# A graph layer's last two stages: relus over two chunks at once, fixed places for t, and an early merge of moments

## The chip, the cores and the metric

The kernel runs on one core of one Trainium2 chip. The metric is the time of one execution on the device, in microseconds (us). A core has a tensor engine (TensorE; PE in the profile, with weight loads as PEld), a vector engine (VectorE, DVE), a scalar engine (ScalarE, ACT), GpSimd (POOL) and a sync engine (SP) that only issues transfers. Each engine works through its own instructions in order and waits on semaphores for the others. Sixteen DMA engines move data between the chip's memory (HBM) and the on-chip SBUF; SP, ACT and POOL issue those transfers from their own queues. Matrix products land in PSUM, from where DVE or ACT take them.

## What is computed

A layer norm with relu, one graph convolution of the GIN kind with two dense layers and two batch norms, and a residual. There are N = 12500 nodes of 256 features, 200000 edges sorted by their target, and a hidden width of 512.

```python
h = jnp.maximum(_layernorm(x, axis=-1), 0.0)
src, dst = (edge_index[0], edge_index[1])
agg = jax.ops.segment_sum(h[src], dst, num_segments=N)
z = (1.0 + eps_gin) * h + agg
t = jnp.dot(z, W1) + b1
t = jax.nn.relu(_batchnorm(t, g1, bt1))
conv_out = jnp.dot(t, W2) + b2
out = jax.nn.relu(_batchnorm(conv_out + h, g2, bt2))
x = x + out
```

A batch norm needs mean and variance over all nodes, so nothing behind it can start before the last node's values are there. That splits the kernel into three stages.

## The kernel before

The nodes are cut into 25 chunks: chunks 0 to 23 have 512 nodes, chunk 24 has 212. Inside the last two stages features lie on the 128 partitions and nodes run along the free dimension; a chunk of y is then a tile of 128 x 2 x 512 (`DC` = 2 halves of the 256 features), a chunk of t is four slices of 128 x 512 (`HC` = 4).

**First stage** (to about 1944 us). For each group of 12 x 128 edges POOL gathers the rows of h with indirect transfers (L529), PE adds them up by target, and the first dense layer follows. Its results, still without batch norm, go to a table in HBM, `t_tab`; h itself, transposed, goes to `h_cols`. The statistics of t are gathered in `st1`. The first eight loads of t slices are already issued in this stage. The change leaves this stage alone.

**The y stage** (about 1947 to 2117 us; the loop `for g in range(NCH)` after `t_load` is defined). For each chunk g:
- ACT applies batch norm 1 and relu to the four slices in place (L809), after their loads have landed;
- ACT issues the load of h for chunk g+3 into y's tile `yT` (L791), and from chunk 1 on one load of a chunk of x for the last stage (`x_load`, `soon`), into ten buffers `xr` and into tiles that are no longer needed (`gtb`, `gta`, `dstT`, `srcT`, `w1s`). Twenty of the 25 chunks of x are loaded here, chunk 24 among them, in a spare part of `dstT`;
- PE multiplies with W2, 8 products in 16 passes (L823);
- SP issues the four loads of chunk g+2's slices (L788). The pool `tin` has `SLICES` = 8 buffers, two chunks' worth, so that each load waits until PE has used the slice two chunks back;
- DVE adds the product to h in `yT` (L830) and takes the statistics of the sum into `st2` (L831).

Then `norm` (L298 to L309) makes scale `sc2` and offset `of2` of batch norm 2: it aggregates the 25 chunks' statistics for each half of the features and does a few tiny operations. `merge` (L282) is a helper that the first batch norm already uses: it aggregates the chunks that are there early and writes the result back as if it were one chunk.

**The tail** (about 2119 us to the end). First SP loads the five chunks of x that had no room before: four into a pool `xmore` that takes the place of `tin`, and chunk 23 into `w2s` (L776). Then for each chunk, 0 to 24 in order, ACT applies scale, offset and relu to the two halves of `yT` in place (L848), PE transposes to rows of nodes with 8 transposes into one PSUM tile `po` (L859), DVE adds that to the chunk of x, in place (L862), and SP stores it to the output (L774; chunk 24 in two stores through `carry`, L353). A store waits for its add; SP's queue holds first the five loads, then the 26 stores in this order.

The order of instructions on each engine in these two stages is that of the code.

Of the kernel before, what the change touches and what calls it, by code (L numbers as in the profile page):

```python
# [15 lines left out]
P = 128  # L16
R = 4
# [9 lines left out]
ACT_PACE = (9, 1)  # L27
SPARE = 4
XIN = 10
XMORE = 4  # L30
SLICES = 8


COPIES = 2
# [6 lines left out]
def kernel(  # L41
# [253 lines left out]
    def norm(pool, st, mv, count, gamma, beta, bias, tag, upto=1):  # L295

        for f in range(count):
            nc.vector.bn_aggr(mv[:, f, :], st[:, f, upto - 1 :, :].rearrange("p g s -> p (g s)"))  # L298
# [10 lines left out]
        nc.vector.tensor_add(of, of, beta)  # L309
        return sc, of  # L310
# [21 lines left out]
    def fast():  # L332
# [24 lines left out]
        with ExitStack() as fs:  # L357
# [398 lines left out]


            late = fs.enter_context(tc.tile_pool(name="late", bufs=1, reuse_waits="tile"))
            yT = [late.tile([P, DC, w * R], F32, name=f"yT{g}") for g, (_, w) in enumerate(chunks)]

            xin = fs.enter_context(tc.tile_pool(name="xin", bufs=XIN, reuse_waits="tile"))
            xrs = {}
# [13 lines left out]
                    eng.dma_start(sb, side)  # L776

            fs.enter_context(tc.manual_schedule())
            with tc.tile_pool(name="tin", bufs=SLICES, side="right", reuse_waits="tile") as tin, tc.tile_pool(
                name="ps_y", bufs=4, space=PSUM  # L780
            ) as ps_y:
                tis = {}

                def t_load(g):
                    n = chunks[g][1] * R
                    for f in range(HC):
                        tis[g, f] = tin.tile([P, CH], F32, name="ti")
# [12 lines left out]
                places += [rows_in(dstT), rows_in(srcT.bitcast(F32)), rows_in(w1s.rearrange("p a b -> p (a b)"))]  # L800
                soon = [(NCH - 1, rows_in(dstT, R * D, len(parts[NCH - 1])))]
                soon = [*enumerate(places)] + soon

                for g in range(2):
                    t_load(g)
                for g in range(NCH):
                    n = chunks[g][1] * R
                    for f in range(HC):
                        nc.scalar.activation(  # L809
                            tis[g, f][:, :n], tis[g, f][:, :n], AF.Relu, bias=of1[:, f : f + 1],  # L810
                            scale=sc1[:, f : f + 1],
                        )
                    for k in range(4) if g == 0 else (g + 3,):
                        if k < NCH:
                            h_load(nc.scalar, k)
                    if soon and g:
                        x_load(nc.scalar, *soon.pop(0))
                    pys = [ps_y.tile([P, CH], F32, name="py") for _ in range(DC)]
                    steps = [(f, d) for f in range(HC) for d in range(DC)]
                    if g == NCH - 1:  # L820
                        steps.sort(key=lambda fd: fd[1])
                    for f, d in steps:
                        nc.tensor.matmul(  # L823
                            pys[d][:, :n], lhsT=w2s[:, f, d * P : (d + 1) * P], rhs=tis[g, f][:, :n],
                            start=(f == 0), stop=(f == HC - 1),
                        )
# [10 lines left out]
            with tc.tile_pool(name="xmore", bufs=XMORE, side="right", reuse_waits="tile") as xmore, tc.tile_pool(  # L837
                name="ps_o", bufs=3, space=PSUM
            ) as ps_o:
                got = len(xrs) - 1  # L840
                assert got + XMORE + 1 == NCH - 1
                for g in range(got, got + XMORE):
                    x_load(nc.sync, g, xmore.tile([P, R, D], F32, name="xr"))
                x_load(nc.sync, NCH - 2, rows_in(w2s.rearrange("p a b -> p (a b)")))
                for g in range(NCH):
                    xt = xrs[g]
                    for d in range(DC):
                        nc.scalar.activation(  # L848
                            yT[g][:, d, :], yT[g][:, d, :], AF.Relu, bias=of2[:, d : d + 1], scale=sc2[:, d : d + 1]
                        )  # L850
                    po = ps_o.tile([P, R, D], F32, name="po")
                    full = len(parts[g]) == R
                    for c, rows in parts[g]:
                        for d in range(DC):
                            if full:
                                nodes = yT[g][:, d, :].rearrange("p (q c) -> p c q", c=R)[:, c, :]
                            else:
                                nodes = yT[g][:, d, c * P : c * P + rows]
                            nc.tensor.transpose(po[:rows, c, d * P : (d + 1) * P], nodes, ident)  # L859
                    for c0, c1, rows in pieces(g):  # L860
                        if c0 < c1:
                            nc.vector.tensor_add(xt[:rows, c0:c1, :], po[:rows, c0:c1, :], xt[:rows, c0:c1, :])  # L862
                    by_four(nc.sync, xt, out, g, store=True)

# [250 lines left out]
```

## Time and profile before

| what | us |
|---|---|
| median of three runs (2167.28 to 2169.49) | 2168.06 |
| the profiled execution, whole | 2167.07 |
| its span, from the first to the last record | 2165.2 |
| y stage: first product to last product | 1947.9 to 2115.9 |
| batch norm 2: last statistics to first relu | 2116.7 to 2119.5 |
| tail: first relu to last relu | 2119.5 to 2154.5 |
| first store issued, last store issued | 2124.2, 2156.9 |

All places in time below are counted from the start of the span. The profile is a record of one execution: each instruction with its start and length, and, worked out from semaphores, what released an engine that had been idle. A group of equal instructions is shown with its busy time and the mean length of one; what stands behind the second bar is the time for which the engine sat idle just before them, and who ended that. Lengths of neighbours on one engine can overlap a little, so the distance from one to the next may be less than the mean length. "DMA share" is the mean busy share of the 16 DMA engines. In this execution the tensor engine was granted 0.87 of its full clock over the whole span, 1.00 in the y stage.

### The profile page before, as it was taken

The page shows a single profiled execution, that of the slowest core. Times are in us where ns is not written, and L with a number is a line of the kernel's source. Part 1 is how long each engine was busy: PE and PEld are TensorE (multiplying, and loading weights), DVE is VectorE, ACT ScalarE, POOL GpSimd, SP SyncE. Part 2 cuts the span into 40 slices and gives each one's busy share as a digit, 9 for nine tenths or more (in the row PEclk, how much of TensorE's full clock was granted, in tenths as well). Part 3 has the DMA queues.
Part 4 walks back from the last instruction along what each step waited for, and adds up shares of the span by engine and source line. Part 5 has one row for each costly group of instructions (what it writes and reads, how often), then busy time and mean ns, then how long its engine had stood idle before and what let it go on. Part 6 is the DMA issues. An engine that isn't in the chain of part 4 may idle for free.

```text
span 2165.2 us, 20953 instructions
## 1 busy us (share of the span) xinstructions
PE 1599.3 (74%) x4874; PEld 981.8 (45%) x4874; DVE 803.0 (37%) x1292; ACT 408.3 (19%) x772; POOL 1464.3 (68%) x1555
## 2 busy tenths in 40 slices
PE   4666767777777777777777777776777777779996
PEld 3454545554444444444444444443444454444445
DVE  5556657552223223223223223323322322323336
ACT  4666667530000000000000000000000000014446
POOL 7777777777777777777777777777777777760000
PEclk9778988988878988889788988898988878999999
DMA  6676877554444444444444444444444444449977
GB/s 198 211 222 223 250 230 233 176 144 126 131 129 135 115 130 136 121 123 136 121 128 132 120 129 131 128 119 131 136 118 126 134 118 123 135 119 314 309 235 288
DMA packets 153845, 349.87 MB, mean 162 GB/s; under 512 B 33564, under 2 KB 63916, under 8 KB 153710
## 3 DMA queue, kind: packets, MB, share of 16 engines
q0 software_dynamic: 74048, 202.28, 33.7%
q1 hardware_dynamic: 42102, 82.38, 11.6%
q10 hardware_dynamic: 37560, 63.76, 8.4%
q8 instruction: 41, 0.67, 0.1%
q14 instruction: 94, 0.77, 0.1%
HBM read 284.29 MB, written 64.00 MB: 161 GB/s over the span
## 4 chain that ended last, share of the span: by engine, by line
POOL 32%; DMA 20%; PE 19%; issue 18%; ACT 6%; DVE 4%; ACTq 0%; DVEq 0%; POOLq 0%
POOL gt L529 28%; PE py L823 8%; PE ps L585 7%; DMA gtb<-h_tab,srcT 6%; DMA gta<-h_tab,srcT 6%; DMA gt<-h_tab,srcT 4%; POOL gta L529 3%; PE ph L626 3%; DMA gt<-in_x_dram,srcT 3%; ACT gt L406 2%; DVE stg L395 2%; ACT yT L848 2%; PE pz L605 2%; ACT gta L406 1%; DMA gta<-in_x_dram,srcT 1%
## 5 line engine op out<-in xcount | busy, mean ns | idle before, releaser
L529 POOL DMA_INDIRECT gt<-h_tab,srcT x708 | 670.7, 947 | 215.9 <-issue 211.0
L585 PE MATMUL ps<-gt,oh 128*128 128x256 f32 x1848 | 619.0, 458 | 242.7 <-DMA gt<-h_tab,srcT 211.6
L585 PEld LDWEIGHTS ps<-gt,oh 128*128 128x128 f32 x1848 | 364.5, 219 | 490.8 <-DMA gt<-h_tab,srcT 341.9
L637 DVE BATCH_NORM_STATS2 st<-ph 128x6 f32<-128x512 f32 (+1 forms) x98 | 67.8, 692 | 946.1 <-PE ph L626 946.0
L529 POOL DMA_INDIRECT gta<-h_tab,srcT x315 | 298.0, 946 | 96.1 <-issue 47.0
L585 PE MATMUL ps<-gta,oh 128*128 128x256 f32 x822 | 258.8, 435 | 69.4 <-DMA gta<-h_tab,srcT 68.5
L639 ACT COPY ts<-ph 128x512 f32<-128x512 f32 (+1 forms) x24 | 13.5, 561 | 1433.7 <-DVE st L637 1433.7
L605 PE MATMUL pz<-at,zs 128*128 128x256 f32 (+1 forms) x524 | 202.3, 528 | 92.5 <-ACT zs L592 85.6
L529 POOL DMA_INDIRECT gt<-in_x_dram,srcT x216 | 204.4, 946 | 65.8 <-issue 60.7
L585 PEld LDWEIGHTS ps<-gta,oh 128*128 128x128 f32 x822 | 161.3, 214 | 171.9 <-DMA gta<-h_tab,srcT 135.3
L585 PE MATMUL ps<-gtb,oh 128*128 128x256 f32 x416 | 162.2, 507 | 96.7 <-DMA gtb<-h_tab,srcT 75.4
L564 DVE TENSOR_TENSOR oh<-col,dstT 128x1536 f32<-128x1536 f32 x131 | 227.6, 1737 | 0.0
L626 PE MATMUL ph<-zc,w1s 128*128 128x512 f32 (+1 forms) x392 | 199.8, 639 | 26.6 <-DVE hc L515 25.7
L605 PEld LDWEIGHTS pz<-at,zs 128*128 128x128 f32 x524 | 139.7, 273 | 135.0 <-ACT zs L592 102.4
L529 POOL DMA_INDIRECT gtb<-h_tab,srcT x160 | 151.5, 947 | 48.8 <-PE ps L585 29.3
L823 PE MATMUL py<-ti,w2s 128*128 128x512 f32 (+1 forms) x400 | 167.9, 582 | 2.9 <-ACT ti L809 2.9
L585 PEld LDWEIGHTS ps<-gtb,oh 128*128 128x128 f32 x416 | 91.3, 243 | 149.7 <-DMA gtb<-h_tab,srcT 76.9
L616 DVE TENSOR_TENSOR zc<-pz,zc 128x512 f32<-128x512 f32 (+8 forms) x187 | 92.6, 518 | 121.7 <-PE pz L605 91.1
L626 PEld LDWEIGHTS ph<-zc,w1s 128*128 128x128 f32 x392 | 79.5, 206 | 92.9 <-issue 53.9
L823 PEld LDWEIGHTS py<-ti,w2s 128*128 128x128 f32 x400 | 75.8, 190 | 95.1 <-issue 86.6
L406 ACT ACTIVATE gt<-gt,nbg,rsg 128x256 f32<-128x256 f32 x216 | 108.1, 586 | 9.0 <-DVE nbg L404 9.0
L809 ACT ACTIVATE ti<-ti,of,sc 128x512 f32<-128x512 f32 (+1 forms) x100 | 76.1, 797 | 86.7 <-DMA ti<-t_tab 73.3
(119 smaller groups left out, 984.7 us busy)
## 6 DMA issues: line engine op xcount, KB each, us to landing
t_tab<-ts ACTq DMA_DIRECT2D x96, 256.0 KB
ti<-t_tab SPq DMA_DIRECT2D x96, 256.0 KB
one_s<-h_tab SPq DMA_DIRECT2D x1280, 1.0 KB
one_a<-h_tab ACTq DMA_DIRECT2D x1280, 1.0 KB
xt<-in_x_dram SPq DMA_DIRECT2D x24, 512.0 KB
h_tab<-ht ACTq DMA_DIRECT2D x24, 512.0 KB
h_cols<-hc SPq DMA_DIRECT2D x24, 512.0 KB
zc<-h_cols SPq DMA_DIRECT2D x24, 512.0 KB
```

The costliest lines, as they stand in the source:

```text
L395: nc.vector.bn_stats(st[:, c : c + 2, :].rearrange("p c s -> p (c s)"), two.rearrange("p c d -> p d c"),)
L406: nc.scalar.activation(slot(to, c), slot(v, c), AF.Relu, bias=nb[:, c : c + 1], scale=rs[:, c : c + 1])
L529: nc.gpsimd.indirect_dma_start(out=slot(ga, t - t0)[:rows], out_offset=None, in_=x if i < LEAD else h_tab, in_offset=bass.IndirectOffsetOn ...
L564: nc.vector.tensor_tensor(ohs[i][:, :n, :], col[:, :P].unsqueeze(1).to_broadcast([P, n, P]), dstT[:, t0 : t0 + n].unsqueeze(2).to_broadcas ...
L585: nc.tensor.matmul(ps, lhsT=oh[:rows, j, :], rhs=fetched[:rows], start=(j == order[0]), stop=(j == order[-1]))
L605: nc.tensor.matmul(pz[:, d, :n], lhsT=zs[:, d * P : (d + 1) * P], rhs=at[:, :n], start=True, stop=True)
L616: nc.vector.tensor_add(side, pz[:, :, a - lo : b - lo], side)
L626: nc.tensor.matmul(ph[:, :n], lhsT=w1s[:, d, f * P : (f + 1) * P], rhs=zc[c][:, d, :n], start=(d == 0), stop=(d == DC - 1),)
L637: nc.vector.bn_stats(st1[:, f, c, :], ph[:, :n])
L809: nc.scalar.activation(tis[g, f][:, :n], tis[g, f][:, :n], AF.Relu, bias=of1[:, f : f + 1], scale=sc1[:, f : f + 1],)
L823: nc.tensor.matmul(pys[d][:, :n], lhsT=w2s[:, f, d * P : (d + 1) * P], rhs=tis[g, f][:, :n], start=(f == 0), stop=(f == HC - 1),)
L848: nc.scalar.activation(yT[g][:, d, :], yT[g][:, d, :], AF.Relu, bias=of2[:, d : d + 1], scale=sc2[:, d : d + 1])
```

## The change

Five edits, all in the y stage and the tail.

1. y's tiles hold two chunks each (`twos`, 128 x 2 x 1024; `yT[g]` is one half of one), and the tail relus two chunks in one operation per half of the features. Chunks 0 and 1 are still done singly.
2. t's slices have two fixed places of four slices (`rings`) for even and odd chunks in place of a pool of eight. Chunk 24's four short slices go to other places: one of their own, `col_i`, and `st1`, which is no longer needed.
3. Four late chunks of x are loaded into the two places as chunks 22 and 23 leave them, in the y stage, in place of the pool `xmore`. Chunk 23's still goes to `w2s`.
4. The statistics of the first 23 chunks are merged after chunk 22's, and batch norm 2 aggregates three entries, the merged one and the last two.
5. The tail begins with chunk 24: DVE applies scale and offset (no relu) to it, and its add takes the relu along. Chunk 0's add and store are split into two halves.

```diff
@@
-            yT = [late.tile([P, DC, w * R], F32, name=f"yT{g}") for g, (_, w) in enumerate(chunks)]
+            twos = [late.tile([P, DC, 2 * CH], F32, name=f"yT{k}") for k in range(NCH // 2)]
+            yT = [twos[g // 2][:, :, g % 2 * CH : (g % 2 + 1) * CH] for g in range(NCH - 1)]
+            yT.append(late.tile([P, DC, chunks[-1][1] * R], F32, name="yT_last"))
@@
-            with tc.tile_pool(name="tin", bufs=SLICES, side="right", reuse_waits="tile") as tin, tc.tile_pool(
-                name="ps_y", bufs=4, space=PSUM
-            ) as ps_y:
+            with tc.tile_pool(name="ps_y", bufs=4, space=PSUM) as ps_y:
+                tin = fs.enter_context(tc.tile_pool(name="tin", bufs=1, side="right", reuse_waits="tile"))
+                rings = [tin.tile([P, HC, CH], F32, name=f"ti{k}") for k in range(2)]
+                short = chunks[-1][1] * R
+                dead = st1.rearrange("p f g s -> p (f g s)")
+                lasts = [tin.tile([P, short], F32, name="ti_last"), col_i.bitcast(F32)]
+                lasts += [dead[:, k * short : (k + 1) * short] for k in range(HC - 2)]
@@
-                        tis[g, f] = tin.tile([P, CH], F32, name="ti")
+                        tis[g, f] = rings[g % 2][:, f, :] if g < NCH - 1 else lasts[f]
@@
                     if g + 2 < NCH:
                         t_load(g + 2)
+                    if g >= NCH - 3 and g < NCH - 1:
+                        for k in range(2):
+                            x_load(nc.sync, len(xrs) - 1, rows_in(rings[g % 2].rearrange("p f n -> p (f n)"), k * R * D))
+                    if g == NCH - 2:
+                        merge(st2, mv2, DC, NCH - 2)
@@
-            sc2, of2 = norm(late, st2, mv2, DC, g2c, bt2c, b2c, "2")
+            sc2, of2 = norm(late, st2, mv2, DC, g2c, bt2c, b2c, "2", NCH - 2)
@@
-                got = len(xrs) - 1
-                assert got + XMORE + 1 == NCH - 1
-                for g in range(got, got + XMORE):
-                    x_load(nc.sync, g, xmore.tile([P, R, D], F32, name="xr"))
                 x_load(nc.sync, NCH - 2, rows_in(w2s.rearrange("p a b -> p (a b)")))
-                for g in range(NCH):
+                for k, g in enumerate([NCH - 1, *range(NCH - 1)]):
                     xt = xrs[g]
                     for d in range(DC):
-                        nc.scalar.activation(
-                            yT[g][:, d, :], yT[g][:, d, :], AF.Relu, bias=of2[:, d : d + 1], scale=sc2[:, d : d + 1]
-                        )
+                        sc, of = sc2[:, d : d + 1], of2[:, d : d + 1]
+                        if k == 0:
+                            nc.vector.tensor_scalar(
+                                yT[g][:, d, :], yT[g][:, d, :], sc, of, op0=OP.mult, op1=OP.add
+                            )
+                        elif g < 2:
+                            nc.scalar.activation(yT[g][:, d, :], yT[g][:, d, :], AF.Relu, bias=of, scale=sc)
+                        elif g % 2 == 0:
+                            two = twos[g // 2][:, d, :]
+                            nc.scalar.activation(two, two, AF.Relu, bias=of, scale=sc)
@@
+                    if k == 1:
+                        side = out[chunks[g][0] : chunks[g][0] + CH, :].rearrange("(p c) d -> p c d", c=R)
+                        for c in range(0, R, 2):
+                            nc.vector.tensor_add(xt[:, c : c + 2, :], po[:, c : c + 2, :], xt[:, c : c + 2, :])
+                            nc.sync.dma_start(side[:, c : c + 2, :], xt[:, c : c + 2, :])
+                        continue
                     for c0, c1, rows in pieces(g):
-                        if c0 < c1:
+                        if c0 == c1:
+                            continue
+                        if k == 0:
+                            nc.vector.scalar_tensor_tensor(
+                                xt[:rows, c0:c1, :], po[:rows, c0:c1, :], 0.0, xt[:rows, c0:c1, :],
+                                op0=OP.max, op1=OP.add,
+                            )
+                        else:
                             nc.vector.tensor_add(xt[:rows, c0:c1, :], po[:rows, c0:c1, :], xt[:rows, c0:c1, :])
                     by_four(nc.sync, xt, out, g, store=True)
```

The order of instructions that results, engine by engine: POOL's is the same. On DVE five instructions of the merge stand between chunk 22's and chunk 23's adds. On SP, before the tail's stores, two x loads wait for chunk 22's products and two for chunk 23's, and w2s's waits for chunk 24's. The loads of h on ACT stand where they stood and now write two runs of 512 elements per partition in place of one of 1024. ACT has 26 relus in the tail in place of 50.

More of the change, by code (lines that the diff above doesn't have):

```diff
@@ L29 @@
 XIN = 10
-XMORE = 4
-SLICES = 8
 COPIES = 2
@@ L758, in fast @@
             late = fs.enter_context(tc.tile_pool(name="late", bufs=1, reuse_waits="tile"))
-            yT = [late.tile([P, DC, w * R], F32, name=f"yT{g}") for g, (_, w) in enumerate(chunks)]
+            assert NCH % 2 and all(w == P for _, w in chunks[:-1])
+            twos = [late.tile([P, DC, 2 * CH], F32, name=f"yT{k}") for k in range(NCH // 2)]
+            yT = [twos[g // 2][:, :, g % 2 * CH : (g % 2 + 1) * CH] for g in range(NCH - 1)]
+            yT.append(late.tile([P, DC, chunks[-1][1] * R], F32, name="yT_last"))
             xin = fs.enter_context(tc.tile_pool(name="xin", bufs=XIN, reuse_waits="tile"))
@@ L832, in fast @@
                 assert not soon
[L834 to L843 removed]
+            sc2, of2 = norm(late, st2, mv2, DC, g2c, bt2c, b2c, "2", NCH - 2)
+            with tc.tile_pool(name="ps_o", bufs=3, space=PSUM) as ps_o:
+                assert len(xrs) == NCH - 1 and NCH - 2 not in xrs
                 x_load(nc.sync, NCH - 2, rows_in(w2s.rearrange("p a b -> p (a b)")))
[L845 removed]
+                for k, g in enumerate([NCH - 1, *range(NCH - 1)]):
                     xt = xrs[g]
                     for d in range(DC):
[L848 to L850 removed]
+                        sc, of = sc2[:, d : d + 1], of2[:, d : d + 1]
[8 more added lines that the diff above has]
+                            nc.scalar.activation(two, two, AF.Relu, bias=of, scale=sc)
                     po = ps_o.tile([P, R, D], F32, name="po")
```

## The prediction

> **What bounds the kernel now.** I read first the chain of waits over the last hundred microseconds, because every edit lies in the last two stages: y (PE product L823, DVE add and statistics L830/L831) and the output tail (ACT relu L848, PE transposes L859, DVE add L862, SP store L774).
>
> ```profile
> 2059.78 56.10 PE py L823 x140
> ...
> 2116.70 1.43 DVE mv L298 x2
> ...
> 2119.54 27.02 ACT yT L848 x39
> ...
> 2147.08 6.47 ACT yT L848 x9
> 2153.59 1.13 PE po L859 x7
> ...
> 2155.88 0.74 DVE dstT L862 x2
> ```
>
> Columns are start, length, engine, tile, line. Until 2115.9 PE alone is the chain: the y stage runs at PE's pace. Then 3.6 us of statistics, and from 2119.5 the tail runs at ACT's pace. The last link is the short chunk 24, which comes after everything else.
>
> Second, the groups by form: busy time and mean ns of one stand behind the bar.
>
> ```profile
> L848 ACT ACTIVATE yT<-yT,of,sc 128x512 f32<-128x512 f32 x48 | 34.0, 803 | 1.1 <-DVE of L309 1.1
> L809 ACT ACTIVATE ti<-ti,of,sc 128x212 f32<-128x212 f32 x4 | 2.3, 563 | 3.5 <-DMA ti<-t_tab 3.5
> L558 ACT ACTIVATE zc<-zc,gin 128x1024 f32<-128x1024 f32 x5 | 5.7, 1132 | 0.0
> L862 DVE TENSOR_TENSOR xr<-po,xr 128x1024 f32<-128x1024 f32 x14 | 17.0, 1223 | 5.4 <-PE po L859 5.3
> L298 DVE BATCH_NORM_AGGREGATE mv<-st 128x2 f32<-128x150 f32 x2 | 1.5, 794 | 0.0
> L298 DVE BATCH_NORM_AGGREGATE mv<-st 128x2 f32<-128x12 f32 x4 | 0.8, 208 | 0.1
> ```
>
> 48 relus take 34.0 us, 0.708 each in a row, so 1.41 per chunk; DVE needs 1.22.
>
> Third, the tail in windows of 2 us (stretch, length, busy PE, PEld, DVE, ACT, POOL, granted clock, DMA share, GB/s), since a faster ACT meets the stores next.
>
> ```profile
> 2128.00:2130.00 2.00, 1.66 (x11) 1.47 (x12) 1.81 (x2) 2.00 (x4) 0.00 (x0) 1.00 1.01 399
> 2144.00:2146.00 2.00, 1.82 (x15) 1.63 (x15) 1.81 (x2) 2.00 (x4) 0.00 (x0) 1.00 0.91 363
> 2148.00:2150.00 2.00, 1.82 (x13) 1.63 (x14) 1.81 (x2) 2.00 (x4) 0.00 (x0) 1.00 0.91 348
> 2158.00:2160.00 2.00, 0.00 (x0) 0.00 (x0) 0.00 (x0) 0.00 (x0) 0.00 (x0) 0.50 0.56 193
> ```
>
> ACT is never idle, but the DMA engines are already at 91 to 101%. While the first four chunks (added 1.21 us apart) were a backlog, 2125.2 to 2132.4, they moved 395 GB/s in mean of the finer windows; later they waited a little for ACT. So ACT is the bound by a small margin, and a store of 524,288 bytes costs 524288/395e9 = 1.33 us of DMA: that is the next bound.
>
> Last, the DMA queues in the middle of y (1980 to 2020): packets, MB, share of 16 engines.
>
> ```profile
> q1 hardware_dynamic: 3407, 6.20, 47.6%
> q10 hardware_dynamic: 1624, 5.92, 42.2%
> ```
>
> q1 is SP's t slices in rows of 2 KB, q10 is ACT's h and x loads in rows of 4 KB. Together 90%: the y stage has one tenth of its DMA time to spare.
>
> **The change part by part.**
>
> *Norm 2.* merge takes 23 chunks out of the last aggregate. Two aggregates of 150 elements (794 ns) become two of 18; between the rows 128x12 (208) and 128x150 the slope is 4.2 ns, so 233 each. On the chain 1.43 us become about 0.45: gain 1.0 (0.9 to 1.1). The merge costs 2 x 0.74 (144 elements: 758 ns) + 0.07 + 0.16 + 0.31 = 2.0 us on DVE, once, after chunk 22's statistics at 2108.05. There DVE idles 4.1 us until PE ends chunk 23, so nothing; without that cover it would be 2.0. ACT's first relu then starts at 2118.5, not 2119.5.
>
> *t's places and x's late chunks.* The slices keep their depth: a load of chunk g+2 waits for the same two products of chunk g. Chunk 24's four short slices get places of their own and wait for none; they gain nothing, because PE reaches them at 2112.8. Four x loads leave the head of the tail (SP issued five at 2114.9 to 2117.3) for the ends of chunks 22 and 23, 2102 to 2112.6, where the DMA share is 0.26 and lower. Behind them on SP stand only w2s's load and the stores, wanted no earlier than 2120.9. Cost nothing; at worst, if all four still stood before the first store, 4 x 1.33 = 5.3 us of DMA would, as before, end near 2123.5, and the gain of the first store below (0.3) would be gone.
>
> *h loads.* y's tiles of two chunks cut each row of 4 KB in two of 2 KB. From the queue rows: q1 took 0.476 x 640 engine-us for 6.20 MB = 49.1 per MB, q10 0.422 x 640 / 5.92 = 45.6. So 0.524 MB x 3.5 = 1.8 engine-us more per chunk, 0.11 us over 16 engines: DMA goes from 6.17 to 6.29 of PE's 6.86 us. Hidden, zero. At the upper end a half row could cost as much as a whole one: see the third rival.
>
> *Relu in pairs.* 4 single relus (chunks 0, 1) stay, 22 of 1024 elements replace 44. No row shows this form. Low end 1.13 us (L558, same size, one operand fewer), high end 1.41 (two single ones, no gain). From 212 to 512 elements the same operation grows by (803-563)/300 = 0.80 ns each, so 803 + 512 x 0.80 = 1.21, less the 0.10 by which neighbours overlap (803 against 708): I take 1.12, 2.24 per two chunks. ACT falls to 1.12 per chunk, under DVE's 1.22 and the store's 1.33. The price: chunk 2 waits for a relu of two chunks.
>
> *Chunk 24 first, chunk 0 in halves.* Chunk 24 gets its scale from DVE, two of about 0.4 us (L597: 286 ns at 84 elements, 393 at 180), four transposes, two adds of 0.42 (L862: 415) with the relu folded in; its two stores go at about 2120.9 and 2121.4, while ACT and PE work toward chunk 0, whose transposes the four short ones (1.0 us at most at the halved clock of this moment) go ahead of. That is hidden behind ACT's first pair; without it, it would be the 1.6 us of DVE. It leaves the end: today w2s's chunk is issued at 2155.99, chunk 24's stores at 2156.42 and 2156.92, and the DMA dies away only at 2160.6. The halves of chunk 0 bring a first store about 1.4 us earlier (2122.8 against 2124.17), of which little remains, as follows.
>
> *The sum.* ACT: 2118.5 + 4 x 0.705 = 2121.3, then the pair of chunks 2 and 3 is done at 2121.3 + 2 x 1.12 = 2123.55. Transposes 1.15, add 1.21: chunk 2's store goes at 2125.95; data flows 0.75 later (2124.17 to about 2124.9 today), at 2126.7, when chunks 0 and 1 are just through. From there 22 chunks are stored at 1.327: 29.2. DVE feeds them each 1.22 to 1.25, ahead of that. I add 0.4 for one short drop like the one near 2133 (0.81 in its 2 us), which now is not caught up, and 0.5 for the last store's uneven engines (0 to 1.4, today's): 2126.7 + 29.2 + 0.4 + 0.5 = 2156.8 against 2160.6. **Gain 3.8 us**: 1.0 norm, about 2.4 chunk 24 gone from the end, 0.4 pace and start. The span goes from 2165.2 to 2161.4, the profiled execution's 2167.07 to 2163.3; that execution lies 1.0 under the median 2168.06 (runs 2167.28 to 2169.49), so the median goes to **2164.3**.
>
> The Trainium skill, "DMA: Bandwidth & Descriptors", section "Bandwidth", puts transfers between HBM and SBUF at a limit of about 358 GB/s per core. By it a store would cost 1.46 us and the tail would end near 2159.4, a gain of 1.2, which is the second rival's case. This trace shows 399 and 393 in two windows in a row, so the limit is not what binds here.
>
> **The rivals.**
>
> *DVE becomes the bound, the stores keep up.* For it: single slices of the tail show 410 to 426 GB/s, which is 1.23 to 1.28 per store. Against: no 2 us show more than 410. Then the last add ends at 2125.9 + 21 x 1.22 = 2151.5, and the last store has landed 0.1 + 0.75 + 1.3 + 0.8 later, 2154.5 to 2155: gain 5.7, 2162.4.
>
> *The pace stays.* Either the stores do no better than the 348 to 385 GB/s of 2140 to 2156 (mean 370, 1.417 per chunk: 2126.7 + 22 x 1.417 + 0.5 = 2158.4, gain 2.2), or the long relu saves nothing (last relu at 2118.5 + 48 x 0.708 = 2152.5, one earlier store: gain 3.0). For it: the DMA share is already 0.94. Against: it was filled to 1.01 when there was a backlog. 2165.5, which counts as no change.
>
> *The h loads starve PE.* The place is L791, the price is the row. The y stage has 6.86 - 6.17 = 0.69 us to spare per chunk, 11 engine-us over 128 rows, 0.086 us per row on top of 0.187. If a 2 KB piece of h costs over 0.137 us, PE waits. At a full doubling a chunk needs 6.17 + 1.5 = 7.67, 0.81 too much, over some 20 chunks 16 us, less 3.8: 2180, slower. For it: ACT's relu of t waits 73.3 us for t's loads and is but 3 to 5 us ahead of PE in mid-stage. Against: t's rows of just that size cost 0.10.
>
> **How the numbers follow.** A measurement of this kernel tells about 0.2%, 4.3 us, from no change. Forecast 0.55, with a range of its own of 3.2 to 4.8 us gain (2163.3 to 2164.9) by 395 or 410 GB/s and the uneven end, two fifths of it over 4.3; DVE-bound 0.17; pace stays 0.20; starved PE 0.08. Faster: 0.17 + 0.23 = 0.40; slower 0.08; same 0.52. The range, 2161.8 to 2166.8, takes in both faster cases and the second rival with a little spread of the runs, and leaves out the starved PE.
>
> **What would show it.** In the new profile: aggregates of 18 elements and the first relu 1.0 us earlier after PE's last product; relus of 1024 elements at 1.1 to 1.2 us; ACT with idle time or done before 2147; the tail's DMA share at 0.97 to 1.0 and SP's stores no longer waiting for DVE in its second half; chunk 24's stores first. Wrong would be: PE idle inside the y stage, t's slices landing later, a DMA share under 0.93 in the tail, or any shift before 1947, where nothing is changed.

## The result, and the profile after

| | before | changed |
|---|---|---|
| median, us (22 runs each) | 2167.76 (2165.61 to 2171.94) | 2163.74 (2160.06 to 2167.34) |
| ratio | | 0.9982 (95%: 0.9976 to 0.9988) |

The changed kernel is about 4.0 us faster (2.6 to 5.2), right at the 0.2% that was called the edge of no change; forecast were 3.8 us and 2164.3. The spans of the two profiled executions add up like this (all from the timelines; the end of the stores' data is the first window of 0.1 us after which nothing flows for 0.8 us):

| stretch, us | before | changed |
|---|---|---|
| start of the span to the first product of y | 1947.9 | 1947.6 |
| first to last product of y | 167.9 | 169.4 |
| last product to first relu | 3.68 | 2.51 |
| first relu to the end of the stores' data | 41.1 | 38.8 |
| from there to the end of the span | 4.6 | 3.4 |
| span | 2165.2 | 2161.7 |

Between the last product and the end of the stores' data 3.4 us are gained. What the first profile lost in the y stage (1.4) and gained at the end (1.2) nearly cancels; run 5 below shows that the loss is no part of the change.

The chain of waits of the changed kernel from the last products on (start, length, what):

```profile
2109.84 7.17 PE py L828 x26
...
2117.83 0.28 DVE mv L296 x2
...
2119.51 1.53 ACT yT L859 x2
...
2121.09 4.80 PE po L871 x23
...
2127.05 8.01 DVE xr L887 x7
...
2149.70 1.21 DVE w2s L887
```

The two aggregates on the chain take 0.28 us, not 1.43. ACT, which held 33 us of the old chain, is on it for 1.5. Then the view names DVE; but what stands behind the last add is 10.8 us long, and there the next views help. The groups by form:

```profile
L862 ACT ACTIVATE yT<-yT,of,sc 128x1024 f32<-128x1024 f32 x22 | 25.0, 1227 | 0.0
L859 ACT ACTIVATE yT<-yT,of,sc 128x512 f32<-128x512 f32 x4 | 2.9, 802 | 1.1 <-DVE of L307 1.1
L887 DVE TENSOR_TENSOR xr<-po,xr 128x1024 f32<-128x1024 f32 x9 | 10.4, 1218 | 0.5 <-PE po L871 0.4
L285 DVE BATCH_NORM_AGGREGATE mv<-st 128x2 f32<-128x138 f32 x2 | 1.4, 740 | 0.0
L296 DVE BATCH_NORM_AGGREGATE mv<-st 128x2 f32<-128x18 f32 x2 | 0.4, 220 | 0.0
```

The merge itself (from 2109.10 to 2110.78) costs nothing, since DVE then still waits for chunk 23's product (in brackets: how long, and for whom):

```profile
2113.31 0.69 DVE L840 TENSOR_TENSOR yT<-py,yT 128x512 f32<-128x512 f32 x1 [2.54 <-PE py L828]
```

A relu of two chunks takes 1.23 us, 25.0/22 = 1.14 in a row: 0.28 less than two single ones. DVE waits for PE only 0.5 us before the nine adds into `xr`, where it waited 5.4 before 14. The tail in windows (the columns as before, granted clock, DMA share and GB/s last):

```profile
2120.00:2122.00 2.00, 1.83 (x9) 1.50 (x10) 0.95 (x3) 2.00 (x4) 0.00 (x0) 0.80 0.00 0
2128.00:2130.00 2.00, 1.94 (x17) 1.75 (x16) 2.00 (x3) 2.00 (x3) 0.00 (x0) 1.00 1.01 408
2144.00:2146.00 2.00, 1.94 (x16) 1.75 (x16) 2.00 (x3) 2.00 (x2) 0.00 (x0) 1.00 1.03 399
2148.00:2150.00 2.00, 1.49 (x13) 1.30 (x11) 2.00 (x3) 0.00 (x0) 0.00 (x0) 1.00 1.02 403
2154.00:2156.00 2.00, 0.00 (x0) 0.00 (x0) 0.00 (x0) 0.00 (x0) 0.00 (x0) 0.50 1.04 403
2156.00:2158.00 2.00, 0.00 (x0) 0.00 (x0) 0.00 (x0) 0.00 (x0) 0.00 (x0) 0.50 0.46 172
2158.00:2160.00 2.00, 0.00 (x0) 0.00 (x0) 0.00 (x0) 0.00 (x0) 0.00 (x0) 0.50 0.03 10
```

From 2126.6, when chunk 1's data begin to flow, the DMA engines are full almost without a break until 2156.4, also after ACT (done at 2147.4) and DVE (2150.9): the stores are the bound there. Ahead of it they idle in part. SP shows the backlog too. Its issue of one store in the kernel before, and of the last stores now (start, length):

```profile
2148.93 0.33 SPq L774 DMA_DIRECT2D out_dram<-w1s  x1
```

```profile
2145.84 1.49 SPq L775 DMA_DIRECT2D out_dram<-w1s  x1
2147.42 5.07 SPq L775 DMA_DIRECT2D out_dram<-ti  x4
2152.59 1.11 SPq L775 DMA_DIRECT2D out_dram<-w2s  x1
```

An issue that took 0.33 us late in the tail of before, at a DMA share of 0.91, now takes 1.1 to 1.6, at a share of 1.01 to 1.04. In the middle of y (1980 to 2020) the queues show the split h rows:

```profile
q1 hardware_dynamic: 3241, 5.90, 43.3%
q10 hardware_dynamic: 2314, 5.93, 42.9%
```

q10, ACT's loads, has 2314 packets in place of 1624 for the same bytes and 42.9% in place of 42.2%: the split rows cost little, and a chunk of y takes 6.86 us as before.

### The profile page after: what moved, and what is told of

It reads as the page before. It is cut to its first block, busy times and chain, and to the rows that moved or that the text cites. A ratio compares the mean times of both kernels' runs of the same rounds, so it can differ in the third digit from the quotient of the medians.

```text
span 2161.7 us, 20849 instructions
## 1 busy us (share of the span) xinstructions
PE 1595.0 (74%) x4874; PEld 974.7 (45%) x4874; DVE 803.0 (37%) x1300; ACT 400.7 (19%) x748; POOL 1463.7 (68%) x1555
## 4 chain that ended last, share of the span: by engine, by line
POOL 32%; DMA 22%; PE 19%; issue 17%; ACT 5%; DVE 4%; ACTq 0%; POOLq 0%; DVEq 0%
POOL gt L527 28%; PE py L828 8%; PE ps L583 7%; DMA gta<-h_tab,srcT 6%; DMA gtb<-h_tab,srcT 6%; DMA gt<-h_tab,srcT 4%; DMA gt<-in_x_dram,srcT 4%; POOL gta L527 3%; ACT gt L404 3%; PE ph L624 2%; PE pz L603 2%; DMA gta<-in_x_dram,srcT 1%; DVE stg L393 1%; ACT gta L404 1%; POOL gta L223 1%
## 5 line engine op out<-in xcount | busy, mean ns | idle before, releaser
L583 PE MATMUL ps<-gt,oh 128*128 128x256 f32 x1848 | 612.6, 454 | 241.7 <-DMA gt<-h_tab,srcT 216.6
L583 PE MATMUL ps<-gta,oh 128*128 128x256 f32 x822 | 264.5, 442 | 69.3 <-DMA gta<-h_tab,srcT 67.8
L583 PE MATMUL ps<-gtb,oh 128*128 128x256 f32 x416 | 157.5, 492 | 99.3 <-DMA gtb<-h_tab,srcT 75.2
L828 PE MATMUL py<-ti,w2s 128*128 128x512 f32 x384 | 166.5, 597 | 2.9 <-ACT ti L814 2.9
L527 POOL DMA_INDIRECT gta<-in_x_dram,srcT x80 | 75.6, 945 | 24.4 <-issue 9.1
```

What stands on the lines that cost most here:

```text
L527: nc.gpsimd.indirect_dma_start(out=slot(ga, t - t0)[:rows], out_offset=None, in_=x if i < LEAD else h_tab, in_offset=bass.IndirectOffsetOn ...
L583: nc.tensor.matmul(ps, lhsT=oh[:rows, j, :], rhs=fetched[:rows], start=(j == order[0]), stop=(j == order[-1]))
L828: nc.tensor.matmul(pys[d][:, :n], lhsT=w2s[:, f, d * P : (d + 1) * P], rhs=tis[g, f][:, :n], start=(f == 0), stop=(f == HC - 1),)
```

## The experiments

Each was timed beside the kernel before on the same chip. A ratio's interval is about as wide as the effects here, so the profiles decide. "Close" is the time from the end of y's last product to the end of the stores' data; "ending" is what is left from there to the end of the span.

| kernel | ratio to before (95%) | close, us | ending | y stage |
|---|---|---|---|---|
| before | | 44.7 | 4.6 | 167.9 |
| changed | 0.9982 (0.9976 to 0.9988) | 41.3 | 3.4 | 169.4 |
| 1 merge alone | 0.9996 (0.9987 to 1.0005) | 43.7 | 4.8 | 169.6 |
| 2 chunk 24 last | 0.9988 (0.9980 to 0.9997) | 42.0 | 4.7 | 167.9 |
| 3 single relus | 0.9988 (0.9980 to 0.9997) | 42.7 | 4.4 | 167.9 |
| 4 three quarters stored | 0.9963 (0.9950 to 0.9976) | 37.1 | 4.5 | 169.6 |
| 5 changed, again | 0.9980 (0.9971 to 0.9989) | 41.2 | 3.3 | 167.9 |
| 6 late x, first try | 0.9986 (0.9977 to 0.9995) | 41.8 | 3.4 | 170.9 |
| 7 14 transposes in the gap | 0.9985 (0.9976 to 0.9994) | 41.4 | 3.3 | 169.6 |
| 8 both gaps, four single relus | 0.9986 (0.9977 to 0.9995) | 42.0 | 3.4 | 167.9 |
| 9 25 transposes in the gap | 0.9973 (0.9964 to 0.9983) | 41.2 | 3.2 | 169.6 |
| 10 late x behind w2s | 0.9984 (0.9975 to 0.9993) | 42.6 | 3.3 | 167.9 |
| 11 stores fed early | 0.9972 (0.9963 to 0.9982) | 40.6 | 3.4 | 167.9 |
| 12 the same, POOL later | 0.9967 (0.9955 to 0.9978) | 40.2 | 3.6 | 167.9 |

Two columns say how to read the first four expectations, which counted to the end of the span (44.7 in the changed kernel). The ending was 4.4 to 4.8 us in runs 1 to 4, which shared a chip, and 3.2 to 3.6 in all later ones, on others; runs 3 and 4 end with the same instructions as the changed kernel, so the order of the chunks does not make it. On which chips the first two profiles (4.6 and 3.4) were taken is not known, so it stays open whether the change has a part in the ending. I therefore read these four by the close, and their expected numbers less 3.4; this way of reading was chosen after they had run, so the number to the end of the span is given too. The close of the changed order of instructions was 41.3, 41.2 and 41.8 in three executions (the changed kernel, runs 5 and 6): differences under 0.6 us say little.

**1, the merge alone on the kernel before.**

```diff
+                    if g == NCH - 2:
+                        merge(st2, mv2, DC, NCH - 2)
...
-            sc2, of2 = norm(late, st2, mv2, DC, g2c, bt2c, b2c, "2")
+            sc2, of2 = norm(late, st2, mv2, DC, g2c, bt2c, b2c, "2", NCH - 2)
```

> The kernel before, with the early merge of batch norm 2's statistics alone (edit 4). Measure: from the end of PE's last product of y to the end of the span, 49.3 us in the profile of before and 44.7 in that of the changed kernel. Theory (the norm's step stands on the chain, and the tail of before is bound by ACT's relus behind it): two aggregates of 150 elements become two of 18, the first relu comes 2.5 us after the last product in place of 3.66, and all of it passes through: 48.1 to 48.3, a time about 1.1 us lower (ratio 0.9995). Rival (the stores, busy to 0.94 in the tail of before, set the end already): the relus start sooner but the end stays, 49.0 to 49.3, ratio 1.000.

ACT's relus of the tail, from the first on:

```profile
2119.65 34.92 ACT L850 ACTIVATE yT<-yT,of,sc 128x512 f32<-128x512 f32 x50 [1.09 <-DVE of L309]
```

The first relu came 2.52 us after the last product (3.68 before), the close was 1.1 us shorter, the time lower by 0.9 with an interval that takes in zero. To the end of the span it is 48.5, just above the theory's 48.1 to 48.3 and under the rival's 49.0. In the old tail, too, the norm's gain passes through almost whole. The theory holds by the profile, not by the time.

**2, chunk 24 last again.**

```diff
-                for k, g in enumerate([NCH - 1, *range(NCH - 1)]):
+                for g in range(NCH):
...
-                        elif g < 2:
+                        if g < 2 or g == NCH - 1:
...
```

> The changed kernel with chunk 24 last again, relued by ACT as in the kernel before; pairs, halves of chunk 0, merge and places stay. Same measure, 44.7 in the changed kernel. Theory of the prediction (chunk 24's issues and stores at the end cost about 2.4 us): 46.8 to 47.3. Rival (the stores bind, so the order is worth only chunk 24's 217,088 bytes at 404 GB/s, 0.54 us, and perhaps half a us for two more issues): 45.2 to 45.7, ratio to before about 0.9987. Third (it does not matter what is last): 44.7.

SP issues chunk 24's two stores last:

```profile
2152.70 2.30 SPq L351 DMA_DIRECT2D out_dram<-dstT  x2
```

To the end of the span it is 46.7, which looks like the theory; but 1.3 of the 2.0 us is the ending. By the close 0.7 us are lost (0.2 to 0.8 against the three executions), the rival's number: with full DMA engines, the order is worth the 217,088 bytes of chunk 24 (0.54 us), and perhaps two issues. The times (0.9988 against 0.9982) can't tell 0.7 from 2.

**3, all relus single.**

```diff
-                        elif g < 2:
+                        else:
                             nc.scalar.activation(yT[g][:, d, :], yT[g][:, d, :], AF.Relu, bias=of, scale=sc)
-                        elif g % 2 == 0:
-                            two = twos[g // 2][:, d, :]
-                            nc.scalar.activation(two, two, AF.Relu, bias=of, scale=sc)
```

> The changed kernel with all relus of the tail done singly, 512 elements; the order with chunk 24 first, the halves of chunk 0, merge and places stay. Same measure, 44.7 in the changed kernel. Theory (stores bind in the changed kernel, ACT with single relus is the next bound at 1.417 us a chunk against 1.30): the last relu ends 34.0 us after the first, the last store lands 4.5 to 5 later, so 0.5 to 1.2 us are lost: 45.2 to 45.9, ratio to before 0.9987. Rival one (the pairs are the main gain, 0.28 us for each of 22 chunks, while before was bound by ACT): 47 or more. Rival two (the stores set the end with either relu): 44.5 to 44.8, nothing lost.

By the close 1.4 us are lost (0.9 to 1.5 against the three executions), a little more than the 0.5 to 1.2 of the theory and less than the 2.3 that rival one put at the least. To the end of the span it is 47.1, rival one's number, of which 1.0 is the ending. As expected, the last relu ended 34.0 us after the first; behind it lay 6.15 us to the end of the data, not 4.5 to 5. Two windows of its tail, and SP's last issue:

```profile
2140.00:2142.00 2.00, 1.71 (x12) 1.33 (x11) 1.62 (x3) 2.00 (x4) 0.00 (x0) 1.00 0.97 387
2148.00:2150.00 2.00, 1.82 (x15) 1.63 (x15) 1.81 (x2) 2.00 (x4) 0.00 (x0) 1.00 0.92 361
```

```profile
2158.60 0.33 SPq L775 DMA_DIRECT2D out_dram<-w2s  x1
```

ACT is busy all the time, the DMA share falls to 0.92 and SP issues in 0.33 us: with single relus ACT is the bound again, by a margin that a chunk feels as 1.417 against 1.30 us.

**4, less to store.** A quarter of the output of chunks 1 to 23 is left out.

```diff
-                    eng.dma_start(side, sb)
+                    eng.dma_start(side[:, : R - 1, :], sb[:, : R - 1, :])
```

> The changed kernel, but the stores of chunks 1 to 23 write three of each four nodes; a quarter of the output of these chunks is left out. All adds and relus stay. Same measure, 44.7 in the changed kernel. Theory (the transfers of the stores set the tail's end): a store takes 0.98 us in place of 1.30, DVE becomes the bound, its last add ends where it does now (33.9 us after the last product) and the store behind it has landed 2.5 later: 39.5 to 40.5, DMA share under 0.85, SP's issues back at 0.3 to 0.5 us. Rival (ACT, DVE or SP's own issuing sets the pace): only the last store is shorter, 44.0 to 44.4.

The close fell by 4.2 us, to 37.1, and the time to 0.9963. All compute is unchanged (the last add ended 33.9 us after the last product, as in the changed kernel). So the transfers of the stores do set the end of the changed kernel. Without that limit ACT and DVE would:

```profile
2134.00:2136.00 2.00, 1.94 (x16) 1.75 (x15) 2.00 (x3) 2.00 (x3) 0.00 (x0) 1.00 0.89 347
2142.00:2144.00 2.00, 1.94 (x17) 1.75 (x16) 2.00 (x3) 2.00 (x3) 0.00 (x0) 1.00 0.74 282
```

DVE and ACT are both at 2.00 of 2 us and the DMA engines have time to spare. ACT's 22 long relus take 25.0 us here, and DVE's adds of the same 22 chunks as long, 1.14 us a chunk each, so it is not shown that DVE alone would be next. By the close the size is at the edge of what was expected (37.1 of 36.1 to 37.1); to the end of the span it is 41.6, not 39.5 to 40.5.

**5, the changed kernel once more**, unaltered.

> The changed kernel once more, unaltered, for two things that one profile can't tell. In its first profile the span ended 3.3 us behind the last store's data, in five other profiles 4.3 to 5.0; and the y stage took 169.4 us with the granted clock at half for 3.5 us of its start, where before took 167.95. Measures: from the end of PE's last product of y to the end of the stores' data (41.4 in the first profile, 44.8 in before) and to the end of the span (44.7). Theory (both are chance from one execution to the next): the data end again at 41.2 to 41.6, the span's end may be at 44.7 to 46.4, and the y stage takes either 167.9 or 169.5. Rival (the change itself shortens the program's ending and slows chunk 0): 44.7 and 169.4 again.

The close is 41.2, the y stage 167.9: the first profile's 1.4 us in y are chance. The ending is 3.3 again, as the rival says; that it goes with the chip rests on the runs above alone.

**6 and 10, where the late loads of x stand.** In run 6 they moved, in the code, from the y loop to the head of the tail:

```diff
-                    if g >= NCH - 3 and g < NCH - 1:
-                        for k in range(2):
-                            x_load(nc.sync, len(xrs) - 1, rows_in(...))
...
+                for q in (NCH - 3, NCH - 2):
+                    for k in range(2):
+                        x_load(nc.sync, len(xrs) - 1, rows_in(...))
                 x_load(nc.sync, NCH - 2, rows_in(w2s.rearrange("p a b -> p (a b)")))
```

> The changed kernel with the four late x loads back at the head of the tail (edit 3 undone as to time; their places stay). Measure: from PE's last product of y to the end of the stores' data, 41.4 in the changed kernel. Theory (the DMA engines idle 2119.6 to 2122 and again near 2124 in the changed kernel, but four loads are 4 x 1.3 = 5.2 us of transfer, so they push the first stores back, and now the stores bind): 42 to 44. Rival (the prediction's: it costs nothing or 0.3, since the loads of 5.2 us end near 2123.5 and chunk 2's store flows at 2126.7): 41.4 to 41.7.

This run tells nothing of the loads: SP has nothing between the two places, so its queue was that of the changed kernel. It is a third execution of it. In run 10 the two `for` lines stand behind w2s's load, which waits for the last product.

> The changed kernel with the four late x loads behind w2s's load in SP's queue, which waits for y's last product: so they do stand in the tail, which they did not in the run meant for it (SP has nothing between the two places, and the order of its instructions was the changed kernel's). Measure as before, 41.2 to 41.8. Theory of the prediction (free as long as they end before the backlog of stores begins: five loads of 1.3 us run from 0.8 to 7.4 after the last product, chunk 24 and chunk 0 take 1.9 more, and chunk 1's store flows at 9.5 in the changed kernel too): 41.2 to 41.8, DMA share near 1 in the first 8 us. Rival (the stores bind, so DMA time spent on loads in the tail is paid for at least in part): 42.5 to 44.

```profile
2116.00:2118.00 2.00, 0.13 (x1) 0.14 (x1) 1.51 (x8) 0.91 (x2) 0.00 (x0) 1.00 0.98 328
2118.00:2120.00 2.00, 1.84 (x13) 1.52 (x12) 0.81 (x3) 2.00 (x4) 0.00 (x0) 0.98 0.96 377
2120.00:2122.00 2.00, 1.94 (x10) 1.58 (x8) 1.29 (x2) 2.00 (x3) 0.00 (x0) 0.50 0.94 340
```

The head of the tail is filled with loads (0.94 to 0.98), and the close grows to 42.6: 0.8 to 1.4 us over the three executions of the changed order. The smaller number is the fairer one: it is against run 6, whose granted clock at the head of the tail was halved for 6.8 us as in this run, and not for 3.4 us as in the other two. The prediction's "free" falls, the rival's range is touched at its low edge. In the kernel before the four stood about 1.5 us earlier (issued from 1.0 us ahead of the last product to 1.0 behind it; here from 0.5 to 2.5 behind it), so I take this as the most that edit 3 can be worth there.

**7 and 9, the halved clock of the tail's head.** In all nine profiles without an edit here the granted clock is halved for 3.4 us (in three of them 6.8) about when chunks 0 and 1 are transposed. PE was given transposes of `ident`, into a PSUM tile that nobody reads, to fill the 3.0 us behind y's last product, 14 in run 7 and 25 in run 9:

```diff
                 assert not soon
+                for _ in range(14):
+                    nc.tensor.transpose(warm, ident, ident)
```

> The changed kernel, and behind the last product of y PE makes 14 transposes of ident into a tile of PSUM that nobody reads, to fill its 3.0 us of idling before the tail. Measure as before, 41.4. Theory (PE's granted clock is halved from 2121.2 to 2124.5 since it idled, which makes chunk 0's and 1's transposes late while the DMA engines wait): the clock stays at 1.00, chunk 1's store is issued about 1 us sooner after the last product than now (8.9), the data end 0.5 to 1.0 sooner: 40.4 to 40.9. Rival one (the halving comes a fixed time after the first stage or by load, not by idling): the clock is halved all the same, 41.4. Rival two (DVE and ACT set the start): clock 1.00, yet 41.2 to 41.5.

> As the run with 14 transposes of ident behind y's last product, but 25 of them: at the 0.121 us that they took each there, they fill the whole of PE's 3.0 us of idling. Measure: from PE's last product of y to the end of the stores' data, 41.3, 41.2 and 41.8 in three executions of the changed kernel's order. Theory (the clock is halved when a stretch of some 3 us had too little on PE; with 14 a gap of 1.5 us was left and it was halved all the same): granted clock 1.00 through the start of the tail, chunk 1's store issued 7.5 to 7.8 us after the last product in place of 8.6 to 8.9; chunk 2's, which waits for a relu of two chunks, hardly sooner, so the data end at 40.8 to 41.1. Rival (transposes do not hold the clock up at all): halved again, 41.2 to 41.8.

With 14 a gap of 1.48 us was left, and the clock was halved all the same. With 25 (2.89 us of transposes, a gap of 0.28) it stayed. Run 7, then run 9, in which the last line is DVE's with its wait:

```profile
2122.00:2124.00 2.00, 1.72 (x8) 1.31 (x7) 1.37 (x2) 2.00 (x3) 0.00 (x0) 0.50 0.82 291
```

```profile
2122.00:2124.00 2.00, 1.23 (x8) 0.85 (x8) 1.72 (x2) 2.00 (x3) 0.00 (x0) 1.00 0.63 235
2124.88 9.15 DVE L891 TENSOR_TENSOR xr<-po,xr 128x1024 f32<-128x1024 f32 x8 [1.04 <-PE po L875]
```

The clock was halved in all eleven executions with a gap of 1.48 us or more (runs 7 and 8 among them), and in none of the three with 0.28 (runs 9, 11 and 12): it is PE's idling that halves it. How much idling it takes is not shown. But the close is 41.2 still: chunk 1's store went 7.9 us after the last product and not 8.6 to 8.9, and then DVE waited 1.04 us for chunk 2, whose transposes need a relu of two chunks. A gain at the head is lost at the next wait. The time, 0.9973, is lower than the close explains. So it is in all three runs on that chip: by their times, runs 9, 10 and 11 gain 1.4 to 2.4 us more than by their closes. The cause is open, so ratios from different chips are not to be compared too finely.

**8, 11 and 12, a version that starts the stores sooner.** Run 8 put transposes into both gaps of PE (14, and 12 ahead of y's first product), relued chunks 2 and 3 singly, and took the transposes of chunks 0 to 3 by halves of the features.

> As the run before it (14 transposes of ident behind y's last product), with 12 more ahead of y's first product; chunks 2 and 3 relued singly too, and the transposes of chunks 0 to 3 take the first half of the features for all four nodes before the second, so that they can start on one relu. Theory (stores bind, so what counts is how early they start; chunk 1's store 1.5 and chunk 2's 1.6 us sooner after the last product than in the changed kernel, at 8.9 and 10.1): the data end 1.2 to 1.6 us sooner, 39.8 to 40.2, the y stage takes 167.9, and the time is 1.5 to 2.5 us under the changed kernel's, ratio to before 0.997. Rival (a later limit, DVE at 1.14 to 1.22 us a chunk, or the stores' rate, takes it back): 40.8 or more.

A miss: the close is 42.0. 14 were too few, the clock was halved, and the later switch to pairs made DVE wait 0.74 us. Run 11 has 25 and 22 transposes, keeps run 8's order of the transposes of chunks 0 to 3, and gives chunk 2's scaling to POOL, idle for 180 us by then:

```diff
...
+                        elif g == 2:
+                            nc.gpsimd.tensor_scalar(
+                                yT[g][:, d, :], yT[g][:, d, :], sc, of, op0=OP.mult, op1=OP.add
+                            )
-                        elif g < 2:
+                        elif g < 4:
...
-                        if k == 0:
+                        if k == 0 or g == 2:
                             nc.vector.scalar_tensor_tensor(
...
```

> A version meant to start the backlog of stores sooner: 25 transposes of ident behind y's last product and 22 ahead of its first (into a PSUM tile that nobody reads), chunk 2's scale and offset on POOL with the relu in its add, chunk 3's relu single, the transposes of chunks 0 to 3 by halves of the features. Theory (stores bind from the first backlog on): chunk 1's store at 7.5 us after the last product, chunk 2's at 8.7 and the next 1.2 apart, so the data flow unbroken from 8.2 and end 8.2 + 23 x 1.30 + 1.9 = 40.0 after it (39.7 to 40.4) in place of 41.2 to 41.8; the y stage takes 167.9; ratio to before 0.9970 to 0.9975. Rival one (POOL needs over 3 us for its two halves): chunk 2's store after 10, 41 or more. Rival two (the clock is halved all the same): 40.8 to 41.5.

The close is 40.6, 0.6 to 1.2 under the changed kernel's and a little over the forecast of 39.7 to 40.4. Run 12 lets POOL start behind DVE's scaling of chunk 24, by a copy of the offsets:

```diff
+                            if d == DC - 1:
+                                nc.vector.tensor_copy(of3, of2)
...
-                                yT[g][:, d, :], yT[g][:, d, :], sc, of, op0=OP.mult, op1=OP.add
+                                yT[g][:, d, :], yT[g][:, d, :], sc, of3[:, d : d + 1], op0=OP.mult, op1=OP.add
```

> As the version that feeds the stores early, but POOL's scaling of chunk 2 takes a copy of the offsets that DVE makes (about 0.16 us) behind its scaling of chunk 24, so that POOL starts only then. In the run before, POOL worked beside that scaling, DVE's two operations took 1.07 us in place of 0.69, and chunk 24's first store went at 4.7 us after y's last product in place of 4.3. Measure: from there to the end of the stores' data, 40.6 in that run, 41.2 to 41.8 in the changed kernel. Theory (the two engines get in each other's way over SBUF, and what is lost at the start is lost at the end): DVE's pair at 0.69 again, chunk 24's first store at 4.3 to 4.5, chunk 1's at 7.3 to 7.5, the data end at 40.2 to 40.5; ratio to before 0.9970 to 0.9975. Rival (the start is not set by that, or POOL now is late): 40.6 or more, DVE's adds of chunk 24 slowed instead.

DVE's line of the timeline in run 11, then in run 12:

```profile
2119.36 1.07 DVE L861 TENSOR_SCALAR yT_last<-yT_last,sc,of 128x212 f32<-128x212 f32 x2
```

```profile
2120.51 0.69 DVE L862 TENSOR_SCALAR yT_last<-yT_last,sc,of 128x212 f32<-128x212 f32 x2
```

The pair is back at 0.69, the first store goes at 4.3 us, the close is 40.2 as forecast. Chunk 1's store, forecast at 7.3 to 7.5, goes at 7.7 as in run 11. The close moved by 0.4 from run 11 to 12, less than it does from one execution to the next, so it is not shown that what is lost at the start is lost at the end. Run 12 has the lowest ratio of all kernels that store the whole output: 0.9967 (0.9955 to 0.9978). Its interval and the changed kernel's still overlap, by 0.0002, so by times alone it is not shown to be faster than the changed kernel; the close is 1.0 to 1.6 us shorter.

## Why the prediction was right

The likeliest case came true: the stores became the bound (run 4), and the gain of 4.0 us (2.6 to 5.2) holds the forecast 3.8. That the numbers came so close is in part luck, as the terms show:

- **Norm, 1.0 forecast.** 1.17 measured between last product and first relu, and the merge, 1.7 us and not 2.0, lay in DVE's wait for chunk 23 (its aggregates read 138 elements, not the 144 of the forecast). Run 1 shows that the gain passes to the end.
- **Tail, 2.8 forecast; 2.3 measured** from first relu to the end of the data. The sum is near, its parts were not. "About 2.4 chunk 24 gone from the end" is the step that was mis-sized: run 2 has 0.7. "0.4 pace and start" was too small: without the pairs 1.4 is lost (run 3). Losses from undoing edits singly need not add up to the whole, and no run undid the halves of chunk 0 or t's places alone, so their share is not known. The mistake was to read the 3.7 us between the last store's issue and the end of its data as chunk 24's price; most of it is paid by whatever comes last (3.7 us again in run 3, where that is chunk 23).
- **The stores' pace.** The start was right: chunk 2's data were forecast to flow 10.8 us after the last product, and chunk 1's flowed at 9.6, so chunk 2's 1.3 later. 1.327 us a store was forecast, and 404 GB/s (mean of the windows from 2128 to 2156) make 1.30, 0.6 less over 22 chunks. The drop for which 0.4 was added did not come. But the uneven end was put at 0.5 and is 1.9: after 2156.4 the data trickle until 2158.3. These errors cancel to 0.4 us by luck.
- **Relu of 1024 elements.** 1.21 forecast by the slope, 1.23 measured; 1.12 in a row, 1.14.
- **h rows.** 0.11 us of DMA a chunk forecast and hidden; by q10's share (0.429 x 640 / 5.93 = 46.3 engine-us per MB for 45.6, over the 1.05 MB of h and x in a chunk) it is 0.05. PE ran through the y stage without idling.
- **Late x loads "cost nothing".** True of where the change puts them. That they cost nothing in the tail either is what run 10 refutes.
- **DVE's adds.** 1.22 to 1.25 a chunk was forecast; in a row they stand 1.13 apart. The overlap of neighbours was taken off for ACT and not for DVE. It cost nothing here, since the stores bind.
- **The rivals.** The first, DVE as the bound, did not occur; DVE and ACT at the same pace are what is left if a quarter of the stores' bytes goes (run 4). The second rival's "long relu saves nothing" is what run 3 imitates: there ACT sets the pace again. Starved PE did not occur. The limit of 358 GB/s of the Trainium skill ("DMA: Bandwidth & Descriptors", "Bandwidth"), weighed in the prediction, is exceeded for 28 us on end (397 to 412 in each window of 2 us). The same section has it as the share of a core while both cores of a pair stream, and this kernel runs on one core.

## What to carry to other kernels

When two engines and the transfers are within 15% of each other, costing each edit for itself misleads: the edits share one bound, and the next wait takes part of what one gains. Undo them one at a time from the finished kernel, and measure between two events of the trace (here last product to last byte), which repeats to 0.6 us where the whole time scatters by 6 to 7: in the 14 profiles the first product of y alone starts anywhere from 1945.9 to 1951.7. When the transfers are the bound, look for idle DMA engines ahead of the backlog, not for faster compute behind it.

## What was not expected of the hardware

- **The clock halves by chance at the start of y.** PE idles 2.9 us there in every run without an edit at this place. In six of these eleven profiles the granted clock then fell to 0.50, in the changed kernel's first profile so:

```profile
1947.00:1948.00 1.00, 0.35 (x1) 0.36 (x2) 0.00 (x0) 1.00 (x2) 0.00 (x0) 0.56 0.01 2
1949.00:1950.00 1.00, 1.00 (x2) 0.33 (x1) 0.00 (x0) 1.00 (x3) 0.00 (x0) 0.50 0.98 377
```

  The y stage takes 167.9 us without it, 169.4 to 169.6 with one dip of 3.3 us, 170.9 with a dip twice as long. In the three with 12 or 22 transposes, which left 2.4 and 1.3 us of the gap, there was none; with 6 of 11 that may still be luck. The Trainium skill ("TensorE: Matmul & The Clock Gate", "Part 1: The HAM clock gate") says that activity is judged in windows of about 3.4 us that run free of the kernel; dips of 3.4 and 6.8 us, now there and now not after the same idling, agree with it. It gives an idle window as the cause of halving; run 7 was halved with no more than 1.5 us of idling in one piece.
- **POOL slows DVE.** Beside POOL's two scalings (1.63 us), DVE's two took 1.07 us in place of 0.69. It is the second that grew, to 0.77 us beside 0.39 for the first; it ended at 2120.43, 0.1 us after POOL's first. The Trainium skill ("SBUF — State Buffer", "SBUF: two separate sides") has the two share a pair of ports that one of them locks; the delay of 0.38 us in run 11, gone in run 12, agrees with it.
- **A backlog shows at its issuer.** SP's issue of a store takes 0.33 us in the late tail of before and of run 3, at DMA shares of 0.91 and 0.92, and 1.1 to 1.6 us in the changed kernel at 1.01 to 1.04. SP looks busy where the transfers are the bound.
